# A fused cross-attention and feed-forward kernel: the order of output projection, down and up within a slot

## The chip, the cores and the metric

The kernel runs on one core of one Trainium2 chip. The time is the device time of one execution in microseconds; it is given as the median of three runs, and beside it stands one further execution that the hardware profiler recorded. The engines are named as in the profile: PE (TensorE, matrix products and transposes), DVE (VectorE), ACT (ScalarE), POOL (GpSimd) and SP (SyncE, which only issues transfers).

## The reference

The block takes `x` (16 batches of 224 tokens of width 512), a context of 16 x 750 rows of width 384 and a mask that leaves out part of the context rows:

```python
# cross attention, 8 heads of 64
q = layernorm(x) @ W_q ; k = context @ W_k ; v = context @ W_v
attn = softmax(where(mask, q k^T / 8, -max))
x = x + tanh(g_xattn) * ((attn v) @ W_o + b_o)
# feed-forward with quantised activations and weights
def bitlinear(x, w, b):              # w: ternary times one scale
    xq = act_quant(rmsnorm(x))       # per row: round(x * 127 / max|x|) / scale
    return xq @ weight_quant(w).T + b
h = gelu(bitlinear(layernorm(x), w1, b1))      # 512 -> 2048
x = x + tanh(g_ffn) * bitlinear(h, w2, b2)     # 2048 -> 512
```

The quantiser of the second product needs the largest magnitude of a whole row of `h` after the Gelu, and its rmsnorm needs the row's sum of squares.

## The kernel before, in words

**Two tilings.** Attention goes by batch: `compact_path` has a loop of 16 *slots*, one batch each (sorted by the number of context rows that the mask leaves; the first 8 slots have room for 192 rows, the last 8 for 128, `CAPS`). Everything after attention goes by *pairs*: 2 x 128 tokens, 14 pairs in all (`NPAIR`). As 224 tokens of a slot are fewer than 256, the pairs fall behind the slots: slot 9 completes no pair.

**Attention of slot s.** `scores(s, n)` for four units n (two halves of the tokens, two groups of heads): matmuls into a wide PSUM tile `sim` (line 1047), the row maximum and masking on DVE (1061, tile `nm`), Exp on ACT (1071), the reciprocal (1080) and the scaling of the probabilities `p` on POOL (1081). `turn_probs` transposes `p` on PE (1101, 1108). `weighted` multiplies with the values (1126, 1141) and ACT copies the result into `xoT` (766), a ring of four slots. Units 0 and 1 of slot s+1 are emitted at the end of slot s; units 2 and 3 in the middle of their own slot. Beside it, slot s prepares slot s+1: keys and values of its context (881, 892, 907, 918) and queries (987, 1008).

**A pair's stages.**
- `residual(i)`: POOL fetches the pair's rows of `x` into `y` (793, tag `y`, three buffers) and adds the bias (1182).
- `project(i, k)` for its two tiles k: `op`, 16 matmul records a pair (1189), then DVE adds it to `y` (1192).
- `normalise(i)`: statistics, subtraction, row maximum and quantisation on DVE (1226 to 1236), a transposing transfer on SP's queue into `xqT` (1237), some small operations and the addition of `b2` to `y` on POOL (1242, 1247).
- `up(i, k, g)`, four groups a pair: 8 matmuls each into a wide PSUM tile `hp` (1259), and DVE evicts them into `h` with scale and bias (1267). `h` has two buffers, one per k.
- `gelu(i, (k,))`: Gelu on ACT (1279), row maximum on DVE (1282), quantisation (1285, 1286), a transposing transfer into `hqT` (1288, two buffers), Square on ACT (1290), five small operations on POOL for the scale c.
- `down(i, k)`: 16 matmuls `fp` a tile (1304), DVE adds to `y` (1308), POOL stores the rows (1310).

**Order.** Each stage is a list of pieces with costs: `project_pieces` 1.8 each and then `normalise` at 0, `up_pieces` 1.8 each with `gelu` at 0 after every second, `down_pieces` 3.5 each. In a slot there are three streams: the attention of this slot, the preparation of the next one, and `flow`, which holds the stages of the pairs. `merge` (1434) emits the next piece of the stream that is least far along in its own total cost, so `flow` is spread over the slot. The emitted order is a priority: the framework then plans the queue of each engine and may put an instruction that is ready ahead of one that isn't. PSUM has two wide tiles (`ps_sim`: `sim`, `hp`, `av`) and four tiles of one bank (`ps_gen`: all else). `evict` gives a copy to DVE or ACT by a running estimate of their loads, which later stages add to.

Slots 0 and 1 have the quantisation of the weights in `flow`. From slot 2 on, before the change, `flow` is: residual(p); up of the pair projected in an earlier slot; projection and normalise of p; down of the pair whose up came just before. So slot 2 has only a projection, slots 3 to 8 have up(p-1), project(p), down(p-1), slot 9 has up(6) alone, slot 10 project(7) and down(6), and slots 11 to 15 again all three. After the loop (line 1540 and on) come the projection of pair 13, up of pair 12, and up of pair 13 woven with the downs of 12 and then 13.

Of the kernel before, what the change touches and what calls it, by code (L numbers as in the profile page):

```python
# [166 lines left out]
def flamingo_gated_kernel(  # L167
# [75 lines left out]
    with tc.If(sh.n_odd == 0) as few:  # L243
        with ExitStack() as stage:
            compact_path(stage, tc, sh, x, context, out, late_loads)
# [480 lines left out]
def compact_path(ctx, tc, sh, x, context, out, late_loads):  # L726
# [4 lines left out]
    _, J, C = context.shape  # L731
# [60 lines left out]
    def fetch_x(dst, t):  # L792
        nc.gpsimd.indirect_dma_start(
            out=dst,
            out_offset=None,
            in_=x_rows,
            in_offset=bass.IndirectOffsetOnAxis(ap=token(t), axis=0),
            bounds_check=B * S - 1,
            oob_is_err=False,
        )  # L800
# [224 lines left out]
    def norm_pieces(s):  # L1025
        pieces = []
        for t in tiles_of(s):
            if t % 2 == 0:
                pieces.append((0.0, lambda t=t: norm(t // 2)))
                if t // 2 + 2 < NTOK // 2:  # L1030
                    pieces.append((0.0, lambda t=t: fetch(t // 2 + 2)))
        return pieces
# [142 lines left out]
    def residual(i):  # L1175

        f = pairs[i] = {}
        f["y"] = y = late["rows"].tile([P, 2, D], F32, tag="y", name=f"y_{i}", bufs=3)
        for k in range(2):
            fetch_x(y[:, k, :], 2 * i + k)  # L1180
        for k in range(2):
            nc.gpsimd.tensor_tensor(y[:, k, :], y[:, k, :], sh.bo, ALU.add)

    def project(i, k):
        y = pairs[i]["y"]
        at = (2 * i + k) * P % RING
        po = gen([P, D], F32, f"op_{i}_{k}")
        for d in range(ND):
            nc.tensor.matmul(  # L1189
                po, lhsT=xoT[:, d, at : at + P], rhs=sh.wo[:, d, :], start=(d == 0), stop=(d == ND - 1)  # L1190
            )
        nc.vector.scalar_tensor_tensor(y[:, k, :], po, sh.tgates[:, 0:1], y[:, k, :], ALU.mult, ALU.add)
        load["v"] += 700
# [56 lines left out]
    def up(i, k, g):  # L1250
        f = pairs[i]
        if g == 0:
            f["h", k] = pa.tile([P, FF], F32, tag="h", name=f"h_{i}_{k}", bufs=2)
        h = f["h", k]
        ph = wide([P, 2, NB], F32, f"hp_{i}_{k}_{g}")
        for n in range(2):
            at = (2 * g + n) * NB
            for d in range(ND):
                nc.tensor.matmul(  # L1259
                    ph[:, n, :],  # L1260
                    lhsT=f["xqT"][:, k * ND + d, :],
                    rhs=w1T[:, d, at : at + NB],
                    start=(d == 0),
                    stop=(d == ND - 1),
                )
        cols = slice(2 * g * NB, 2 * (g + 1) * NB)
        nc.vector.scalar_tensor_tensor(  # L1267
            h[:, cols], ph.rearrange("t i n -> t (i n)"), f["c1", k], sh.b1[:, cols], ALU.mult, ALU.add
        )
        load["v"] += 1280  # L1270
# [29 lines left out]
    def down(i, k):  # L1300
        f = pairs[i]
        po = gen([P, D], F32, f"fp_{i}_{k}")
        for n in range(NF):
            nc.tensor.matmul(  # L1304
                po, lhsT=f["hqT", k][:, n, :], rhs=w2T[:, n, :], start=(n == 0), stop=(n == NF - 1)
            )
        y = f["y"][:, k, :]
        nc.vector.scalar_tensor_tensor(y, po, f["c2", k], y, ALU.mult, ALU.add)  # L1308
        load["v"] += 700
        nc.gpsimd.indirect_dma_start(  # L1310
            out=out_rows,
            out_offset=bass.IndirectOffsetOnAxis(ap=token(2 * i + k), axis=0),
            in_=y,
            in_offset=None,
            bounds_check=B * S - 1,
            oob_is_err=False,
        )
# [3 lines left out]
    def up_pieces(i):  # L1321
        p = []
        for k in range(2):
            p += [(1.8, lambda g=g, k=k: up(i, k, g)) for g in range(2)]
            p.append((0.0, lambda k=k: gelu(i, (k,))))
        return p

    def down_pieces(i):
        return [(3.5, lambda k=k: down(i, k)) for k in range(2)]

    def project_pieces(i):
        p = [(1.8, lambda k=k: project(i, k)) for k in range(2)]
        return p + [(0.0, lambda: normalise(i))]
# [116 lines left out]
    def weave(a, b):  # L1450

        outl = []
        ia = ib = 0
        while ia < len(a) or ib < len(b):
            if ib >= len(b) or (ia < len(a) and ia * len(b) <= ib * len(a)):
                outl.append(a[ia])
                ia += 1
            else:
                outl.append(b[ib])
                ib += 1  # L1460
        return outl
# [42 lines left out]
    projected = raised = lowered = 0  # L1504
    for s in range(B):
        other = norm_pieces(s + 2) if s + 2 < B else []
        if s + 2 < B:
            other.append((0.0, lambda s=s: gather(s + 2)))
        if s + 3 < B:
            other.append((0.0, lambda s=s: select(s + 3)))  # L1510
        if s + 1 < B:
            other += weave(context_pieces(s + 1), query_pieces(s + 1))
        flow = []
        if s < 2:
            flow = weight_pieces(s)
        else:
            complete = 256 * (projected + 1) <= S * s
            if projected == 0:
                nc.gpsimd.tensor_scalar(sh.bo, sh.bo, sh.tgates[:, 0:1], None, ALU.mult)
                nc.gpsimd.tensor_scalar(sh.b2, sh.b2, sh.tgates[:, 1:2], None, ALU.mult)  # L1520
            if complete:
                flow.append((0.0, lambda i=projected: residual(i)))
            if raised < projected:
                flow += up_pieces(raised)
                raised += 1
            if complete:
                flow += project_pieces(projected)
                projected += 1
                if lowered < raised:
                    flow += down_pieces(lowered)  # L1530
                    lowered += 1
        merge(attention_pieces(s), other, flow)
        if s == 1:

            late["stage"].close()
            late["rows"] = ctx.enter_context(tc.tile_pool(name="rows", bufs=1))
        if s + 1 < B:
            scores(s + 1, 0)
            scores(s + 1, 1)

    i = NPAIR - 1
    residual(i)
    for k in range(2):
        project(i, k)
        normalise(i, (k,))
    downs = down_pieces(i - 1) + down_pieces(i)
    for _, piece in up_pieces(i - 1):
        piece()
    for _, piece in weave(up_pieces(i), downs[:2]) + downs[2:]:
        piece()  # L1550


# [32 lines left out]
```

## Time and profile before

| | us |
|---|---|
| median of 3 runs | 762.57 (758.72 to 763.36) |
| profiled execution | 755.32 |
| its span, first to last instruction | 753.5 |
| slots 0 and 1 with all that leads in | 115.3 |
| slots 2 to 14 | 536.0 |
| slot 15 | 34.1 |
| after the loop | 68.1 |

| engine | busy us | share of the span |
|---|---|---|
| PE | 680.1 | 90% |
| DVE | 505.9 | 67% |
| ACT | 407.6 | 54% |
| POOL | 397.0 | 53% |

The slots are cut here where the matmuls of their first scores begin on PE, so a stretch ends where the next slot's `sim` starts. A group's line in the profile gives the source line, engine, operation, output and input tiles with shape and count, then busy time and the mean in ns of one, then the idle time just ahead of it on its engine and what ended it. Lines of 766 and 763 are those of `evict`, on ACT and DVE.

### The profile page before, as it was taken

The page shows a single profiled execution, that of the slowest core. Times are in us where ns is not written, and L with a number is a line of the kernel's source. Part 1 is how long each engine was busy: PE and PEld are TensorE (multiplying, and loading weights), DVE is VectorE, ACT ScalarE, POOL GpSimd, SP SyncE. Part 2 cuts the span into 40 slices and gives each one's busy share as a digit, 9 for nine tenths or more (in the row PEclk, how much of TensorE's full clock was granted, in tenths as well). Part 3 has the DMA queues.
Part 4 walks back from the last instruction along what each step waited for, and adds up shares of the span by engine and source line. Part 5 has one row for each costly group of instructions (what it writes and reads, how often), then busy time and mean ns, then how long its engine had stood idle before and what let it go on. Part 6 is the DMA issues. An engine that isn't in the chain of part 4 may idle for free.

```text
span 753.5 us, 11378 instructions
## 1 busy us (share of the span) xinstructions
PE 680.1 (90%) x3902; PEld 432.9 (57%) x3902; DVE 505.9 (67%) x1300; ACT 407.6 (54%) x960; POOL 397.0 (53%) x543
## 2 busy tenths in 40 slices
PE   4997799999999999997999999999999999988652
PEld 3875587666566566555655575666666666443221
DVE  5598765877484784665768676588594939586860
ACT  1556564384663855736657369266565656460530
POOL 6583567464564644647266564565654453536141
PEclk9998999999999999999999999999999999999887
DMA  6874031132223322222142323123122222213150
GB/s 193 314 267 156 11 90 45 15 73 56 69 47 70 82 56 57 67 57 81 28 99 67 71 67 68 32 77 80 58 57 70 56 70 57 71 28 77 35 113 31
DMA packets 87218, 58.77 MB, mean 78 GB/s; under 512 B 75488, under 2 KB 75632, under 8 KB 87024
## 3 DMA queue, kind: packets, MB, share of 16 engines
q1 hardware_dynamic: 79024, 32.00, 18.8%
q0 software_dynamic: 8128, 25.96, 11.1%
q8 instruction: 33, 0.54, 0.3%
q14 instruction: 33, 0.27, 0.1%
HBM read 32.26 MB, written 7.34 MB: 53 GB/s over the span
## 4 chain that ended last, share of the span: by engine, by line
PE 57%; DVE 12%; issue 10%; POOL 9%; DMA 5%; ACT 2%; POOLq 0%; ACTq 0%; DVEq 0%; SPq 0%
PE qp L1008 9%; PE op L1189 9%; PE fp L1304 8%; PE hp L1259 6%; PE kp L892 5%; PE sim L1047 4%; PE vp L907 4%; PE ptp L1101 3%; PE av L1126 3%; DVE a L1282 2%; POOL p L1081 2%; DVE h L1267 2%; DMA raw<-in_L_ffn_w_dram 2%; DMA hqT<-hq 2%; DVE hq L1285 1%
## 5 line engine op out<-in xcount | busy, mean ns | idle before, releaser
L1081 POOL TENSOR_TENSOR p<-p,rec 112x768 f32<-112x768 f32 (+1 forms) x64 | 84.2, 1318 | 74.8 <-DVE rec L1080 29.6
L1304 PE MATMUL fp<-w2T,hqT 128*128 128x512 fp8e4 x448 | 104.2, 387 | 13.8 <-DMA hqT<-hq 13.7
L1259 PE MATMUL hp<-w1T,xqT 128*128 128x512 fp8e4 x448 | 107.0, 383 | 8.8 <-DVE h L1267 6.2
L1071 ACT ACTIVATE p<-p,nm 112x192 f32<-112x192 f32 (+1 forms) x256 | 106.4, 419 | 11.5 <-DVE nm L1061 11.3
L1008 PE MATMUL qp<-xnT,wq_sb 128*128 128x224 f32 x512 | 104.9, 358 | 0.6 <-ACT xnT L766 0.6
L1189 PE MATMUL op<-wo_sb,xoT 128*128 128x512 f32 x224 | 103.7, 599 | 0.0
L1008 PEld LDWEIGHTS qp<-xnT,wq_sb 128*128 128x128 f32 x512 | 96.8, 193 | 6.4 <-issue 3.3
L1267 DVE SCALAR_TENSOR_TENSOR h<-hp,c,b_bc 128x1024 f32<-128x1024 f32 x56 | 71.6, 1280 | 39.9 <-PE hp L1259 37.4
L1061 DVE CUSTOM_DVE_ANT_0 p<-sim,mask 112x192 f32<-112x192 f32 (+1 forms) x256 | 67.7, 319 | 33.9 <-PE sim L1047 33.4
L1304 PEld LDWEIGHTS <-hqT 128*128 128x128 bf16 x448 | 43.3, 99 | 71.0 <-DMA hqT<-hq 16.9
L1282 DVE TENSOR_REDUCE a<-h 128x1 f32<-128x2048 f32 x28 | 63.9, 2282 | 22.4 <-ACT h L1279 22.3
L1259 PEld LDWEIGHTS <-xqT 128*128 128x128 bf16 x448 | 43.2, 98 | 57.7 <-issue 15.4
L1308 DVE SCALAR_TENSOR_TENSOR y<-fp,c,y 128x512 f32<-128x512 f32 x28 | 20.9, 746 | 76.3 <-PE fp L1304 73.0
L1310 POOL DMA_INDIRECT out_dram<-y,token x28 | 30.9, 1104 | 75.6 <-DVE y L1308 70.6
L1290 ACT ACTIVATE h<-h 128x2048 f32<-128x2048 f32 x28 | 53.4, 1907 | 22.1 <-DVE hq L1285 14.7
L1279 ACT ACTIVATE h<-h 128x2048 f32<-128x2048 f32 x28 | 53.5, 1909 | 19.6 <-DVE k L1200 10.6
L1189 PEld LDWEIGHTS op<-wo_sb,xoT 128*128 128x128 f32 x224 | 40.6, 190 | 38.9 <-issue 36.4
L892 PE MATMUL kp<-ctxT,wk_sb 128*128 128x192 f32 (+1 forms) x384 | 60.9, 306 | 0.0
L892 PEld LDWEIGHTS kp<-ctxT,wk_sb 128*128 128x128 f32 x384 | 55.2, 192 | 6.2 <-issue 4.3
L1247 POOL TENSOR_TENSOR y<-y,b_bc 128x512 f32<-128x512 f32 x28 | 36.6, 1311 | 37.9 <-DVE fx L1228 37.6
L766 ACT COPY pT<-ptp 128x448 f32<-128x448 f32 x63 | 32.7, 536 | 42.6 <-PE ptp L1101 41.3
L1101 PE MATMUL ptp<-ident,p 112*128 112x112 f32 x256 | 36.1, 268 | 17.6 <-POOL p L1081 17.5
(165 smaller groups left out, 1191.4 us busy)
## 6 DMA issues: line engine op xcount, KB each, us to landing
raw<-in_L_ffn_w_dram SPq DMA_DIRECT2D x16, 512.0 KB, 5.6
wq_sb<-in_L_xattn_W_q_dram SPq DMA_DIRECT2D x1, 1024.0 KB, 5.8
b_bc<-in_L_ffn_b_dram SPq DMA_DIRECT2D x1, 1024.0 KB, 7.8
wk_sb<-in_L_xattn_W_k_dram SPq DMA_DIRECT2D x1, 768.0 KB, 7.4
wv_sb<-in_L_xattn_W_v_dram SPq DMA_DIRECT2D x1, 768.0 KB, 8.8
wo_sb<-in_L_xattn_W_o_dram SPq DMA_DIRECT2D x1, 512.0 KB, 3.8
wo_sb<-in_L_xattn_W_o_dram SPq DMA_DIRECT2D x2, 256.0 KB, 5.6
x<-in_x_dram,token POOLq DMA_INDIRECT x28, 3.6
```

What stands on the lines that cost most here:

```text
L892: nc.tensor.matmul(pk[:, p - p0, :], lhsT=sh.wk[:, c, p * P : (p + 1) * P], rhs=st["ctxT"][:, c, :cap], start=(c == 0), stop=(c == NC - 1),)
L1008: nc.tensor.matmul(pq[:, i, :], lhsT=sh.wq[:, d, (p + i) * P : (p + i + 1) * P], rhs=st["xnT"][:, d, :], start=(d == 0), stop=(d == ND - 1),)
L1061: nc.vector.tensor_tensor_reduce(out=probs[:, h, :cap], in0=sim[:, j, i, :cap], in1=st["mask"][:, j * begin : j * begin + cap], scale=-(DH ...
L1071: nc.scalar.activation(probs[:, h, :cap], probs[:, h, :cap], AF.Exp, bias=nmax, scale=-1.0, accum_out=total[:TQ, h : h + 1],)
L1081: nc.gpsimd.tensor_tensor(probs[:, :, :cap], probs[:, :, :cap], rec[:TQ].unsqueeze(2).to_broadcast([TQ, 4, cap]), ALU.mult,)
L1101: nc.tensor.transpose(pt[:, h, :], probs[:, h, c : c + P], ident[:TQ, :TQ])
L1189: nc.tensor.matmul(po, lhsT=xoT[:, d, at : at + P], rhs=sh.wo[:, d, :], start=(d == 0), stop=(d == ND - 1))
L1259: nc.tensor.matmul(ph[:, n, :], lhsT=f["xqT"][:, k * ND + d, :], rhs=w1T[:, d, at : at + NB], start=(d == 0), stop=(d == ND - 1),)
L1267: nc.vector.scalar_tensor_tensor(h[:, cols], ph.rearrange("t i n -> t (i n)"), f["c1", k], sh.b1[:, cols], ALU.mult, ALU.add)
L1279: nc.scalar.activation(f["h", k], f["h", k], AF.Gelu)
L1282: nc.vector.tensor_reduce(amax[:, k : k + 1], h, AX.X, ALU.max, apply_absolute_value=True)
L1304: nc.tensor.matmul(po, lhsT=f["hqT", k][:, n, :], rhs=w2T[:, n, :], start=(n == 0), stop=(n == NF - 1))
```

## The change

In a slot, a pair's projection comes first, then down of the pair in front of it, then up of the pair itself. Up thus runs in the slot of its own projection. Down is no longer tied to a slot that completes a pair: it runs whenever the pair in front has been through up. After the loop, up of pair 12 is not left over, and what remains after the projection of pair 13 is emitted as down(12), up(13), down(13).

```diff
             if complete:
                 flow.append((0.0, lambda i=projected: residual(i)))
+                flow += project_pieces(projected)
+                projected += 1
+            if lowered < raised:
+                flow += down_pieces(lowered)
+                lowered += 1
             if raised < projected:
                 flow += up_pieces(raised)
                 raised += 1
-            if complete:
-                flow += project_pieces(projected)
-                projected += 1
-                if lowered < raised:
-                    flow += down_pieces(lowered)
-                    lowered += 1
         merge(attention_pieces(s), other, flow)
...
     for k in range(2):
         project(i, k)
         normalise(i, (k,))
-    downs = down_pieces(i - 1) + down_pieces(i)
-    for _, piece in up_pieces(i - 1):
-        piece()
-    for _, piece in weave(up_pieces(i), downs[:2]) + downs[2:]:
+    for _, piece in down_pieces(i - 1) + up_pieces(i) + down_pieces(i):
         piece()
```

After it, slot 2 has project(0), up(0); slots 3 to 8 have project(p), down(p-1), up(p); slot 9 has down(6) alone; slot 10 has project(7), up(7); slots 11 to 15 again have all three.

## The prediction

> **What bounds the kernel now.** First I read the busy shares, then the costliest groups with what ended their idle time.
>
> ```profile
> PE 680.1 (90%) x3902; PEld 432.9 (57%) x3902; DVE 505.9 (67%) x1300; ACT 407.6 (54%) x960; POOL 397.0 (53%) x543
> L1304 PE MATMUL fp<-w2T,hqT 128*128 128x512 fp8e4 x448 | 104.2, 387 | 13.8 <-DMA hqT<-hq 13.7
> L1259 PE MATMUL hp<-w1T,xqT 128*128 128x512 fp8e4 x448 | 107.0, 383 | 8.8 <-DVE h L1267 6.2
> L1101 PE MATMUL ptp<-ident,p 112*128 112x112 f32 x256 | 36.1, 268 | 17.6 <-POOL p L1081 17.5
> ```
>
> TensorE (PE) is busy for 90%. The next view says where the other 10% lies: busy time of every engine by stretch, cut where the scores of a slot begin (columns: stretch, length, PE, weight loads, DVE, ACT, POOL, granted clock). Shown are slots 2, 4, 7, 9, 11 and 14, then slot 15, then what follows the loop (the tail).
>
> ```profile
> 115.30:147.20 31.90, 31.80 (x203) 22.65 (x201) 21.52 (x72) 12.65 (x44) 20.28 (x23) 1.00 0.17 30
> 194.00:242.80 48.80, 46.99 (x268) 29.56 (x268) 32.62 (x77) 29.48 (x65) 27.79 (x37) 1.00 0.28 66
> 339.20:389.20 50.00, 45.06 (x251) 27.51 (x249) 30.44 (x78) 27.57 (x62) 27.27 (x36) 0.97 0.28 62
> 430.30:459.30 29.00, 27.19 (x176) 18.56 (x175) 19.62 (x56) 22.46 (x55) 16.27 (x21) 1.00 0.27 71
> 491.60:532.60 41.00, 39.94 (x226) 24.83 (x225) 32.18 (x78) 23.16 (x56) 24.13 (x35) 1.00 0.30 69
> 612.10:651.30 39.20, 39.08 (x214) 24.54 (x213) 27.30 (x67) 22.53 (x54) 18.60 (x27) 1.00 0.25 61
> 651.30:685.40 34.10, 27.48 (x146) 13.75 (x146) 25.18 (x65) 20.02 (x47) 17.49 (x23) 1.00 0.31 64
> 685.40:753.50 68.10, 38.90 (x145) 15.80 (x143) 38.37 (x51) 16.72 (x13) 19.00 (x41) 0.83 0.26 58
> ```
>
> Slots 2 to 14 last 536.0 us with 521.6 us of PE work: only 14.4 us idle in thirteen slots. Slot 15 idles for 6.6 us and the tail for 29.2, at a clock of 0.83. PE order in the tail (start, duration, count, idle before):
>
> ```profile
> 685.36 7.03 PE L1189 MATMUL op<-wo_sb,xoT 128*128 128x512 f32 x16
> 692.23 5.43 PE L1259 MATMUL hp<-w1T,xqT 128*128 128x512 fp8e4 x24
> 698.08 5.34 PE L1259 MATMUL hp<-w1T,xqT 128*128 128x512 fp8e4 x24 [0.42 <-DVE k L1200]
> 708.85 1.01 PE L1259 MATMUL hp<-w1T,xqT 128*128 128x512 fp8e4 x2 [5.44 <-DVE h L1267]
> 710.48 5.23 PE L1304 MATMUL fp<-w2T,hqT 128*128 128x512 fp8e4 x16 [0.62 <-DMA hqT<-hq]
> 715.54 3.18 PE L1259 MATMUL hp<-w1T,xqT 128*128 128x512 fp8e4 x14
> 718.86 3.63 PE L1304 MATMUL fp<-w2T,hqT 128*128 128x512 fp8e4 x16
> 731.49 8.42 PE L1304 MATMUL fp<-w2T,hqT 128*128 128x512 fp8e4 x32 [8.99 <-DMA hqT<-hq]
> ```
>
> The tail is P(13), U(12), U(13) mixed with D(12), D(13); P, U, D stand for projection, up and down of a pair. Its waits are for the two buffers of h (5.44) and for hqT (8.99). So inside the slots PE sets the pace, and after them latency does.
>
> **What the Trainium skill says.** "TensorE: Matmul & The Clock Gate", Architectural detail, says that ACT and DVE queues are strict FIFOs, so a reduce that waits for a Gelu holds all that is queued behind it on DVE. The trace agrees in kind: PE waited 5.44 us for an h eviction that stood behind others on DVE. "ScalarE: Activation LUTs", What ACT_TABLE_LOAD costs, gives 1283 ns for a load; the trace has 37 loads for Gelu and Exp of 1283 ns. "Perfetto Trace Analysis", Matmuls, wants independent groups to rotate through PSUM banks; here sims, hp and av rotate through two wide tiles and all else through four.
>
> **The change, part by part.** Prices of one pair on PE, start to start: P 6.87 us (685.36 to 692.23). An fp tile takes 3.46 (673.56 to 677.02 in slot 15), so D is 6.92. An hp group of 8 takes 1.73, so U is 6.92.
>
> Nothing is added or removed: same matmuls, Gelus, transposes and stores. U(p) moves one slot earlier, behind P(p) and D(p-1) in P's own slot.
>
> *Slot 2* gains U(0), 6.92 us; PE is 31.8 of 31.9 busy there, so all of it shows: **+6.9**. Slots 3 to 8 and 11 to 14 hold one P, U and D each, as before. Slot 9 has D(6) for U(6) and slot 10 U(7) for D(6), equal on PE.
>
> *Slot 15 and tail.* From 651.3 to the end are 102.2 us. Nominal PE work: 27.5 in slot 15 and 6.87 + 4 x 6.92 = 34.55 in the tail, 62.0. After the change U(12) runs in slot 15 where U(11) ran, and the tail is P, D, U, D: 62.0 - 6.92 = 55.1. Before, U(13) was done at 718.86, after 67.6 us, with 51.7 us of work behind it (all but D(13) and half of D(12)), so 15.9 were lost: 6.6 idle in slot 15, 6.5 idle and 2.8 of slow clock in the tail. From there to the end were 34.6 us: eviction, Gelu, reduce, quantise, transpose, D(13), store. After it, U(13) is done once 55.1 - 6.9 = 48.2 us of work and the new losses are over. Those I estimate from rows. D(11) finds hqT ready, made at the end of slot 14. U(12) waits for xqT(12): P ends 8 us into the slot, normalise is 5.7 us on DVE (sum of its rows), the transpose lands in 3.1, shared with the scores on DVE: ready at about 20 us, where work without it lasts about 17; loss 3. D(12) waits for hqT(12): Gelu 1.91, reduce 2.28, quantise 1.8, cast 0.8 and landing 4.3 are 11 us against P(13)'s 6.87; loss 4, part of which U(13) fills. I take 5, with 2 and 12 as ends (12: nothing gained on the waits of before). The closing 34.6 becomes 33: hqT of the last pair's first tile took 7.0 us to land beside the store of D(12), against a median of 4.3, and that store now lies earlier. Sum 48.2 + 5 + 33 = 86.2, against 102.2: **-16.0**. With slot 2: **-9**; ends -13 and -1.
>
> *Inside the slots*, cost zero, with covers named. (a) P opens a slot and needs y. The y fetch is not late: in slot 1 three pairs were fetched ahead; the third buffer runs about a slot ahead, and its fetch waits for a store:
>
> ```profile
> 196.82 1.07 POOL L793 DMA_INDIRECT y<-in_x_dram,token  x1 [2.02 <-DMA out_dram<-y,token]
> ```
>
> That store now falls in mid-slot, so POOL's fetch and its two adds of 1.27 us leave the slot's start, where POOL's p multiplications are due. (b) xqT(p) must be there for U(p): done near 20 us after the start by the working above, while P, D, scores and the next slot's queries and keys give PE some 24 us. SP's transpose for xqT now has hqT of U(p-1) in front of it, landed by then. (c) hqT(p) has until D(p), most of half a slot; before it had P's 7 us plus what lay between, and lost little (0.93 in slot 7). If cover (b) fails, PE waits up to 3 us a slot; in slot 10, without a D, most likely. (d) The Gelu chain of U's second tile, 1.91 + 2.28 + 1.43 + 0.80 us on ACT and DVE, ends up beside the next slot's first scores, instead of beside the middle scores. Queued behind its reduce on DVE are the row maxima, behind its Gelu on ACT the Exps; POOL's p and PE's transposes wait for these. Before, these transposes ran 9 to 13 us after the slot's start; the scores need about 8. P and D fill PE meanwhile. On POOL, U's five small operations for c (1.5 us in all) wait for ACT's Square; those of its second tile now stand about where the next slot's p stands, which at worst waits for a Square of 1.91 us. D's two stores (1.1 us of POOL each) move from the slot's end to its middle, where POOL idles. Bounds for (a) to (d) together: -8 (over half of the 14.4 idle goes, as ptp's waits for POOL shrink) to +8 when the covers hold; I take 0. (e) The greedy choice of the evicting engine sees U(0)'s load earlier; a few copies of 0.5 us go from DVE to ACT in slots 2 and 3: nothing.
>
> Against the profiled execution of 755.3 us (span 753.5) this is 746. That run lies 7.3 under the median of 762.6; I put the same difference on the median: **754**.
>
> **Rivals.**
> *Slots lose at their seam* (slower). By (d), the first scores of a slot stand behind the Gelu chain, and the two wide tiles pass from hp to sims only as DVE evicts. For it: slot 7 shows the form, ptp waiting 3.47 us for POOL's p with a Gelu chain beside it. Against: PE now has P, ready, to run there. Price: 1 to 3.5 us in each of thirteen slots; at 2, 26 - 9 = +17: 780. It decides from 9 / 13 = 0.7 us a slot.
> *The tail gives nothing that slot 2 doesn't take* (no change). D(12) waits in full for hqT(12), U(13) behind it; loss 12, so -1, and the planner's new order costs a few us: 763. For it: slot 15 lost 6.6 with the same lack of filling work. Against: two stages of latency less.
> *The slots gain too.* Scores no longer meet two Gelus in mid-slot, table loads fall, ptp's 17.5 us shrink: -9 - 8: 745.
>
> **How the numbers follow.** Chances: forecast (749 to 759) 0.45, slots gain (741 to 749) 0.15, no gain (759 to 769) 0.17, seam (769 to 795) 0.23. One per cent is 7.6 us, about what a measurement of this kernel can tell from no change. Faster than 754.9 is all of the gain case and over half of the forecast: 0.40; slower than 770.2 the seam case: 0.23; the rest 0.37. The range cuts some 0.05 below and 0.12 above: 743 to 779.
>
> **What would show it.** Right: slot 2 near 39 us, other slots within 1 us; slot 15 and tail about 86 with PE order P, D, U, D; no hp wait on h of 5 us; fewer than 37 Gelu and Exp loads. Wrong: longer slots with ptp or hp waiting, DVE's maxima behind L1282 (seam), hp waiting for xqT (cover b), or a tail of 95 us and over.

## The result and the profile after

The changed kernel takes **763.5 us** in the median of 20 runs (758.7 to 767.3), the kernel before 758.6 us in 20 runs beside them (753.0 to 763.4): a ratio of 1.0063, 95% interval 1.0040 to 1.0085. It is slightly slower; forecast was 1.1% faster (754 against 762.6). The first three runs of the kernel before, on whose median of 762.6 the forecast was put, lay high.

The profiled executions are 755.3 and 764.7 us, spans 753.5 and 763.0. The spans lie 9.5 us apart, the medians 4.9, since that of before was quicker than its median and that of after slower. The accounts below are made in these spans.

First the busy shares and groups of the page of after:

```profile
PE 686.7 (90%) x3902; PEld 438.8 (58%) x3902; DVE 509.0 (67%) x1296; ACT 392.9 (52%) x952; POOL 396.0 (52%) x543
L1304 PE MATMUL fp<-w2T,hqT 128*128 128x512 fp8e4 x448 | 110.3, 403 | 19.9 <-DMA hqT<-hq 19.9
L1259 PE MATMUL hp<-w1T,xqT 128*128 128x512 fp8e4 x448 | 104.2, 379 | 6.2 <-DMA xqT<-xq 4.8
```

The same 3902 matmuls take 6.6 us longer on PE, and `fp` waits 19.9 us for hqT instead of 13.7. `hp` waited mostly for DVE's evictions before (6.2 of 8.8); now it is mostly for xqT (4.8 of 6.2). Next the busy times by stretch, cut as before, for slots 2, 4, 7, 9, 10, 14, 15 and the tail:

```profile
114.34:157.24 42.90, 39.68 (x235) 25.83 (x233) 27.66 (x71) 17.94 (x52) 19.79 (x22) 1.00 0.09 23
203.44:250.97 47.53, 45.97 (x270) 29.46 (x269) 30.94 (x78) 26.82 (x63) 27.56 (x37) 1.00 0.31 68
346.93:395.10 48.17, 45.72 (x249) 28.20 (x247) 31.38 (x77) 24.03 (x60) 25.14 (x33) 0.93 0.27 65
435.46:469.08 33.62, 29.18 (x177) 19.38 (x176) 14.69 (x57) 19.10 (x52) 17.57 (x27) 0.90 0.32 79
469.08:506.09 37.01, 34.69 (x200) 22.41 (x199) 24.01 (x74) 16.43 (x50) 15.10 (x19) 1.00 0.07 19
626.88:667.11 40.23, 39.00 (x214) 24.29 (x213) 27.86 (x68) 22.66 (x54) 18.72 (x27) 1.00 0.25 60
667.11:701.26 34.15, 28.99 (x146) 14.09 (x146) 25.36 (x64) 19.80 (x46) 13.95 (x23) 0.95 0.25 55
701.26:763.00 61.74, 32.76 (x113) 13.13 (x111) 32.88 (x47) 13.52 (x11) 17.54 (x36) 0.77 0.27 57
```

All slots together, from both traces ("idle" is the length less PE's busy time):

| stretch | before: length (idle) | after: length (idle) | difference | forecast |
|---|---|---|---|---|
| slots 0, 1 | 115.3 | 114.3 | -0.9 | 0 |
| slot 2 | 31.9 (0.1) | 42.9 (3.2) | +11.0 | +6.9 |
| slots 3 to 8 | 283.1 (11.1) | 278.2 (7.6) | -4.9 | 0 |
| slots 9 to 11 | 102.3 (2.9) | 109.6 (7.4) | +7.3 | 0 |
| slots 12 to 14 | 118.7 (0.3) | 122.1 (3.3) | +3.3 | 0 |
| slot 15 and tail | 102.2 (35.8) | 95.9 (34.1) | -6.3 | -16.0 |
| sum | 753.5 | 763.0 | +9.5 | -9.1 |

The order of PE in the tail of after (start, duration, count, idle before):

```profile
701.26 7.03 PE L1189 MATMUL op<-wo_sb,xoT 128*128 128x512 f32 x16
709.53 3.63 PE L1304 MATMUL fp<-w2T,hqT 128*128 128x512 fp8e4 x16 [1.24 <-DMA hqT<-hq]
717.11 5.31 PE L1304 MATMUL fp<-w2T,hqT 128*128 128x512 fp8e4 x16 [3.96 <-DMA hqT<-hq]
722.26 7.07 PE L1259 MATMUL hp<-w1T,xqT 128*128 128x512 fp8e4 x32
739.39 9.88 PE L1304 MATMUL fp<-w2T,hqT 128*128 128x512 fp8e4 x32 [10.05 <-DMA hqT<-hq]
```

P, D, U, D as foreseen, but D(12) stalls twice, at a clock of 0.77 over the tail, and its second tile and D(13) run below full speed (5.31 and 9.88 us for one and two tiles, where the first tile takes 3.63).

The two slots at which late waits appear. Slot 9, which has D(6) alone, and the U of slot 10:

```profile
437.69 0.69 PE L1047 MATMUL sim<-kT,qT 64*112 64x128 f32 x8 [1.03 <-DVE h L1267]
439.13 1.54 PE L1047 MATMUL sim<-kT,qT 64*112 64x128 f32 x16 [0.75 <-DVE nm L1061]
442.62 6.34 PE L1304 MATMUL fp<-w2T,hqT 128*128 128x512 fp8e4 x16 [1.95 <-DMA hqT<-hq]
...
496.45 5.35 PE L1259 MATMUL hp<-w1T,xqT 128*128 128x512 fp8e4 x24 [2.32 <-DMA xqT<-xq]
```

In slot 9 nothing fills PE while the scores wait for the two wide tiles and D(6) for its hqT; the clock falls and the first half of D(6) takes 6.34 us instead of 3.6. In slot 10 PE has no D to run while the normalise of pair 7 goes through DVE and SP.

### The profile page after: what moved, and what is told of

Its sections match the earlier page's. It is cut to its first block, busy times and chain, and to the rows that moved or that the text cites. A ratio compares the mean times of both kernels' runs of the same rounds, so it can differ in the third digit from the quotient of the medians.

```text
span 763.0 us, 11354 instructions
## 1 busy us (share of the span) xinstructions
PE 686.7 (90%) x3902; PEld 438.8 (58%) x3902; DVE 509.0 (67%) x1296; ACT 392.9 (52%) x952; POOL 396.0 (52%) x543
## 4 chain that ended last, share of the span: by engine, by line
PE 66%; DVE 12%; DMA 6%; ACT 4%; POOL 4%; issue 3%; DVEq 0%; POOLq 0%; ACTq 0%; SPq 0%
PE fp L1304 12%; PE hp L1259 11%; PE qp L1008 10%; PE op L1189 9%; PE kp L892 5%; PE av L1126 4%; DVE a L1282 3%; PE vp L907 3%; PE sim L1047 3%; PE ptp L1101 3%; DMA hqT<-hq 2%; DMA raw<-in_L_ffn_w_dram 2%; ACT h L1279 2%; DVE h L1267 1%; DVE hq L1285 1%
## 5 line engine op out<-in xcount | busy, mean ns | idle before, releaser
L1081 POOL TENSOR_TENSOR p<-p,rec 112x768 f32<-112x768 f32 (+1 forms) x64 | 83.4, 1304 | 94.5 <-DVE rec L1080 66.7
L1304 PE MATMUL fp<-w2T,hqT 128*128 128x512 fp8e4 x448 | 110.3, 403 | 19.9 <-DMA hqT<-hq 19.9
L1071 ACT ACTIVATE p<-p,nm 112x192 f32<-112x192 f32 (+1 forms) x256 | 106.8, 420 | 29.1 <-DVE nm L1061 28.6
L1189 PE MATMUL op<-wo_sb,xoT 128*128 128x512 f32 x224 | 108.4, 624 | 7.6 <-DVE keys L833 5.1
L1259 PE MATMUL hp<-w1T,xqT 128*128 128x512 fp8e4 x448 | 104.2, 379 | 6.2 <-DMA xqT<-xq 4.8
L1304 PEld LDWEIGHTS <-hqT 128*128 128x128 bf16 x448 | 45.2, 103 | 77.0 <-DMA hqT<-hq 22.1
L1061 DVE CUSTOM_DVE_ANT_0 p<-sim,mask 112x192 f32<-112x192 f32 (+1 forms) x256 | 69.7, 314 | 15.0 <-PE sim L1047 12.0
L1259 PEld LDWEIGHTS <-xqT 128*128 128x128 bf16 x448 | 42.5, 98 | 60.1 <-issue 10.9
L1282 DVE TENSOR_REDUCE a<-h 128x1 f32<-128x2048 f32 x28 | 63.9, 2281 | 14.8 <-ACT h L1279 14.8
L1290 ACT ACTIVATE h<-h 128x2048 f32<-128x2048 f32 x28 | 53.4, 1908 | 29.7 <-DVE hq L1285 20.9
L1292 POOL TENSOR_SCALAR r<-ss 128x1 f32<-128x1 f32 x28 | 5.4, 191 | 117.5 <-ACT h L1290 116.5
L892 PEld LDWEIGHTS kp<-ctxT,wk_sb 128*128 128x128 f32 x384 | 58.0, 199 | 3.8 <-issue 1.4
L1047 PE MATMUL sim<-kT,qT 64*112 64x192 f32 (+1 forms) x512 | 51.3, 316 | 5.2 <-DVE nm L1061 4.0
L766 ACT COPY qT<-qp 128x448 f32<-128x448 f32 x30 | 15.9, 528 | 66.5 <-PE qp L1008 66.3
L1047 PEld LDWEIGHTS sim<-kT,qT 64*112 64x112 f32 x512 | 37.1, 173 | 21.8 <-issue 8.6
```

What stands on the lines that cost most here:

```text
L892: nc.tensor.matmul(pk[:, p - p0, :], lhsT=sh.wk[:, c, p * P : (p + 1) * P], rhs=st["ctxT"][:, c, :cap], start=(c == 0), stop=(c == NC - 1),)
L1047: nc.tensor.matmul(sim[:, j, i, :cap], lhsT=st["qT"][j * DH : (j + 1) * DH, p, q * TQ : (q + 1) * TQ], rhs=st["kT"][j * DH : (j + 1) * DH, ...
L1061: nc.vector.tensor_tensor_reduce(out=probs[:, h, :cap], in0=sim[:, j, i, :cap], in1=st["mask"][:, j * begin : j * begin + cap], scale=-(DH ...
L1071: nc.scalar.activation(probs[:, h, :cap], probs[:, h, :cap], AF.Exp, bias=nmax, scale=-1.0, accum_out=total[:TQ, h : h + 1],)
L1081: nc.gpsimd.tensor_tensor(probs[:, :, :cap], probs[:, :, :cap], rec[:TQ].unsqueeze(2).to_broadcast([TQ, 4, cap]), ALU.mult,)
L1189: nc.tensor.matmul(po, lhsT=xoT[:, d, at : at + P], rhs=sh.wo[:, d, :], start=(d == 0), stop=(d == ND - 1))
```

## The experiments

Ratios are to the kernel before, with their 95% intervals; slot lengths are from each kernel's one trace. All edits are to the changed kernel, unless it says otherwise. A median is of 14 to 22 executions, but of 6 for "down only beside a projection" and "all three", and of 5 for "scores first, ctxT on DVE". The rows with 757.7, with 756.5 and with 759.7 or 759.4 in the last column come from three chips, so small steps of the ratio from one of these groups to another are not read as effects.

| run | ratio | median us | before beside it |
|---|---|---|---|
| late switch | 1.0053 (1.0031 to 1.0075) | 761.5 | 757.7 |
| tail woven | 1.0028 (1.0006 to 1.0049) | 761.1 | 757.7 |
| down only beside a projection | 1.0107 (1.0073 to 1.0142) | 765.7 | 757.7 |
| kernel before, tail unwoven | 0.9994 (0.9971 to 1.0017) | 757.5 | 757.7 |
| scores first | 0.9977 (0.9956 to 0.9998) | 755.6 | 756.5 |
| early slots only | 1.0061 (1.0041 to 1.0082) | 761.3 | 756.5 |
| short maximum | 0.9991 (0.9971 to 1.0012) | 756.0 | 756.5 |
| late switch, scores first, woven | 1.0016 (0.9993 to 1.0040) | 758.0 | 756.5 |
| scores first, woven | 0.9927 (0.9903 to 0.9951) | 754.1 | 759.7 |
| scores first, ctxT on DVE | 0.9899 (0.9865 to 0.9934) | 751.8 | 759.7 |
| all three | 0.9863 (0.9824 to 0.9902) | 750.1 | 759.7 |
| kernel before, ctxT on DVE | 1.0020 (0.9993 to 1.0048) | 761.2 | 759.4 |

My theory after the traces: the work went where it was to go, and the waits that were priced at zero (seam, slot 9, slot 10, tail) ate the gain. The rivals: that the tail or slot 2 alone decides; that an early part of the change loses and a late one gains.

### Where in the program: late slots alone, early slots alone

```diff
+            if s < 10:
+                if complete:
+                    flow.append((0.0, lambda i=projected: residual(i)))
+                if raised < projected:
+                    flow += up_pieces(raised)
...
+            else:
+                if complete:
+                    flow.append((0.0, lambda i=projected: residual(i)))
+                    flow += project_pieces(projected)
...
```

> The old order up to slot 9, the new one from slot 10 on: slot 2 has only P(0), slot 9 only U(6), slot 10 has P(7), D(6), U(7), then P, D, U; the end is that of the changed kernel. Theory 'sparse slots' (the loss lies in slots 2, 9 and 10, where P and U, or D, stand without a partner to cover their latency): against the kernel before, slot 10 pays U(7) at its PE time of 6.9 us and nothing else, slots 2 and 9 are as before, slot 15 and tail keep the 6.4 us gained; sum about +1, ratio 1.000 to 1.003, and hp no longer waits for xqT. Rival 'full slots' (each slot in the new order loses at its seam): slots 11 to 14 carry a third of the loss, ratio 1.002 to 1.004 and slots 11 to 14 longer by over 1 us each. Rival 'U(0) alone' (it is the extra 6.9 us of up in an early slot and nothing else): same total as the changed kernel, 1.006, as the 6.9 us are only moved to slot 10.

Ratio 1.0053: the +1 us of 'sparse slots' missed, and by the total alone this is the changed kernel again, as the third reading has it. Slot 2 is at 31.9 and slot 9 at 29.1 again. Slot 10 now has P, D and U and is 7.7 us longer than before, of which 6.9 is the U that moved. Slots 11 to 14 are 42.6, 41.2, 40.7 and 40.2: 4.9 us longer than before. Slot 15 and the tail are 94.5, 7.7 below before. So the tail returns about what one U costs in PE time (6.92), and beside that four ordinary slots lose 4.9 us, as 'full slots' has it.

The counterpart has the new order up to slot 8, the old one from slot 9, and the old end:

```diff
+            if s < 9:
+                if complete:
+                    flow.append((0.0, lambda i=projected: residual(i)))
+                    flow += project_pieces(projected)
...
+            else:
+                if complete:
+                    flow.append((0.0, lambda i=projected: residual(i)))
+                if raised < projected:
+                    flow += up_pieces(raised)
...
-    for _, piece in down_pieces(i - 1) + up_pieces(i) + down_pieces(i):
+    downs = down_pieces(i - 1) + down_pieces(i)
+    for _, piece in up_pieces(i - 1):
         piece()
+    for _, piece in weave(up_pieces(i), downs[:2]) + downs[2:]:
+        piece()
```

> The new order up to slot 8 and the old one from slot 9 on, with the old end; slot 9 then has no share. It shows the early half of the change alone. By the windows of the changed kernel: slot 2 +11.0, slots 3 to 8 -4.9 against before; slot 9 as in the run with down beside a projection, +1.8 (31 us, though it has 7 us less PE work); slots 10 to 14 and the end as before. Sum +8, ratio 1.008 to 1.012. Rival (U(0)'s time comes back where a later slot has less to do): +4 or less, ratio under 1.006.

Ratio 1.0061, below the forecast of 1.008 and at the edge of its rival. Slot 2 is 42.9 and slots 3 to 8 sum to 275.0, 8.1 below before. Slots 10 to 14, in the old order, sum to 192.1 (192.0 before; 198.0 in the changed kernel), and slot 15 with the tail is 102.3. So of the 10.7 us that slots 9 to 14 lose in the changed kernel, the 6.0 of slots 10 to 14 belong to the new order in them, not to what came earlier, and the wide slots do gain. Slot 9 is another matter: it has no share here, 7 us less of PE work than before, and still takes 29.7 us (29.0 before), 6.6 of them idle. No half of the change wins by itself: each has to pay U's 6.9 us where it begins.

### Slot 9: no share at all

```diff
-            if lowered < raised:
+            if complete and lowered < raised:
```

> The changed kernel, but down runs only in a slot that completes a pair: slot 9 has no share at all, slot 10 has P(7), D(6), U(7). Theory 'sparse slots': slots 9 and 10 together take 63 to 65 us instead of 70.6 (61.3 in the kernel before), slot 2 stays at 43; ratio to before 0.997 to 1.001. Rival 'full slots': slots 9 and 10 gain less than 3 us as slot 9 has even less to hide its scores behind; ratio 1.005 or more.

Missed: ratio 1.0107, the slowest of all. Lines of PE in its slot 9:

```profile
434.70 0.69 PE L1047 MATMUL sim<-kT,qT 64*112 64x128 f32 x8 [0.49 <-DVE h L1267]
439.85 1.12 PE L987 MATMUL xnp<-ident,x 128*128 128x128 f32 x4 [2.17 <-DVE k L1200]
446.35 1.01 PE L1101 MATMUL ptp<-ident,p 112*128 112x112 f32 x4 [2.80 <-POOL p L1081]
447.15 5.62 PE L1008 MATMUL qp<-xnT,wq_sb 128*128 128x224 f32 x16
```

Slot 10 no longer waits for xqT, since D(6) fills PE there: its 2.3 us are gone. But without any share slot 9 idles for 6.6 us at a clock of 0.78, takes 30.8 us for 24.2 us of busy time, and slot 11 grows from 38.9 to 42.5. The three slots are 112.0, against 109.6. Behind a slot in the new order, slot 9 idles with D(6) in it (4.4 us) and without (6.6); before, with U(6), it idled for 1.8.

### The tail: its order, and DVE

```diff
-    for _, piece in down_pieces(i - 1) + up_pieces(i) + down_pieces(i):
+    downs = down_pieces(i - 1) + down_pieces(i)
+    for _, piece in weave(up_pieces(i), downs[:2]) + downs[2:]:
```

> The changed kernel, but after the loop up(13) is woven with down(12), as it was before, then down(13). If U(13) is late because it stands behind D(12) on PE, which waits for hqT(12): U(13)'s first groups run ahead of D(12)'s second tile, the end comes 3 to 4 us earlier than in the changed kernel, ratio to before about 1.002. If U(13) is late because xqT(13) itself is late (normalise of pair 13 shares DVE with the Gelu chain of U(12); in the changed kernel xqT lands at 720, U(13) starts at 722): at most 1 us, ratio 1.005 to 1.007.

Ratio 1.0028; the tail is 60.0 instead of 61.7. U(13) now may pass the second half of D(12):

```profile
707.32 3.63 PE L1304 MATMUL fp<-w2T,hqT 128*128 128x512 fp8e4 x16 [1.27 <-DMA hqT<-hq]
714.90 2.46 PE L1304 MATMUL fp<-w2T,hqT 128*128 128x512 fp8e4 x6 [3.96 <-DMA hqT<-hq]
717.60 5.85 PE L1259 MATMUL hp<-w1T,xqT 128*128 128x512 fp8e4 x24 [0.24 <-DMA xqT<-xq]
```

It passes and gains little: U(13) starts 18.6 us after the tail's beginning instead of 21.0, the moment its xqT has landed, and idle time in the tail stays at 28.3 (28.9). The ratio lies nearer to the first forecast (1.002) than to the second (1.005 to 1.007); the 1.7 us of the tail lie between the two. What is left is not PE's order. DVE has to normalise pair 13 and quantise pair 12 at the same time: in the changed kernel it works without a gap of over 0.15 us from 699.4 to 718.2, and xqT(13) lands at 719.8.

```diff
-    downs = down_pieces(i - 1) + down_pieces(i)
-    for _, piece in up_pieces(i - 1):
-        piece()
-    for _, piece in weave(up_pieces(i), downs[:2]) + downs[2:]:
+    for _, piece in up_pieces(i - 1) + down_pieces(i - 1) + up_pieces(i) + down_pieces(i):
```

> The kernel before, with only its end unwoven: up(12), down(12), up(13), down(13) in this order. It separates the order at the end from the depth of the pipeline. If D(12) ahead of U(13) makes PE wait for hqT(12) (2.7 to 4 us a tile in the changed kernel): 4 to 8 us slower than before, ratio 1.005 to 1.010. If the end is bound by DVE and the last Gelu chain whatever PE's order: within 1 us, ratio 0.999 to 1.001.

The edit is to the kernel before, and there, too, the order at the end hardly counts: 0.9994, tail 69.5 (68.1).

The last run on the tail shortens DVE's work. To the woven tail is added an edit that takes the row maximum of pair 12 over 256 of its 2048 columns, so this kernel leaves out a part of the computation:

```diff
+            part_h = h[:, :256] if i == NPAIR - 2 else h
-            nc.vector.tensor_reduce(amax[:, k : k + 1], h, AX.X, ALU.max, apply_absolute_value=True)
+            nc.vector.tensor_reduce(amax[:, k : k + 1], part_h, AX.X, ALU.max, apply_absolute_value=True)
```

> The run with the woven end, and for pair 12 alone the row maximum after Gelu is taken over 256 of 2048 columns (this leaves out part of a computation; each reduce falls from 2.28 to about 0.35 us on DVE). Theory 'DVE at the end' (U(13) starts late because normalise of pair 13 shares DVE with the Gelu chain of U(12)): xqT(13) and U(13) come 3 to 4 us earlier after the loop, the stretch after the loop falls from 60.0 to 56 to 57 us, ratio to before 0.997 to 1.000 (woven end: 1.003). Rival 'chain' (projection, statistics and transfer of pair 13 set it, whatever else is on DVE): under 1 us, ratio about 1.002.

```profile
709.63 3.41 PE L1305 MATMUL fp<-w2T,hqT 128*128 128x512 fp8e4 x15 [1.79 <-DMA hqT<-hq]
712.88 5.34 PE L1259 MATMUL hp<-w1T,xqT 128*128 128x512 fp8e4 x24
```

(The edit shifts the later line numbers by one.) One such reduce takes 0.41 us instead of 2.27; two are 3.7 us less on DVE, and the tail falls by 4.2, to 55.8. U(13) starts 15.5 us after the tail's beginning instead of 18.6. The rival (the chain of pair 13 sets it, whatever else is on DVE) falls: DVE sets the pace there.

### The seam between slots

What follows is slot 7 of the changed kernel, on DVE, from where the second unit of scores is due. L1061 is the masking with its row maximum, which frees the wide tile of a unit; L1282, 1285 and 1286 are maximum, quantisation and cast of h from U's second tile.

```profile
349.26 2.29 DVE L1282 TENSOR_REDUCE a<-h 128x1 f32<-128x2048 f32 x1 [0.46 <-ACT h L1279]
...
352.41 1.28 DVE L1285 TENSOR_SCALAR hq<-h,k 128x2048 int16<-128x2048 f32 x1
353.61 0.17 DVE L1080 RECIPROCAL rec<-sum 112x4 f32<-112x4 f32 x1
353.69 0.33 DVE L1061 CUSTOM_DVE_ANT_0 p<-sim,mask 112x192 f32<-112x192 f32 x1
353.94 2.00 DVE L1286 CAST hq<-hq 128x2048 bf16<-128x2048 int16 x1
355.86 0.34 DVE L1061 CUSTOM_DVE_ANT_0 p<-sim,mask 112x192 f32<-112x192 f32 x1
```

Three long DVE instructions, 5.6 us together, stand among the maxima. PE waits behind them with the next unit of scores:

```profile
356.27 0.98 PE L1047 MATMUL sim<-kT,qT 64*112 64x192 f32 x2 [2.45 <-DVE nm L1061]
357.18 6.48 PE L1189 MATMUL op<-wo_sb,xoT 128*128 128x512 f32 x8
```

In slots 4 to 6 it is the second half of P that waits, 1.6 to 1.8 us each, for a PSUM bank that `keys` (L833, row numbers for the gather of context) frees, behind the same instructions. This is the queue discipline that the Trainium skill states in "TensorE: Matmul & The Clock Gate", Architectural detail: DVE works strictly in order. To test it, the Gelu piece of U's second tile is held back until the first scores of the next slot have been emitted:

```diff
+    held_gelu = []
...
-                flow += up_pieces(raised)
+                flow += up_pieces(raised)[:-1]
+                held_gelu.append(lambda i=raised: gelu(i, (1,)))
...
             scores(s + 1, 0)
             scores(s + 1, 1)
+        while held_gelu:
+            held_gelu.pop()()
```

> The changed kernel, with the Gelu piece of the second tile of an up held back until the first scores of the next slot have been emitted, so that these no longer stand behind it on ACT and DVE. Theory 'seam' (in slots that lack work to cover it, and by 1.2 us in each of slots 12 to 14, PE waits because Exp and the copies on ACT stand behind the last Gelu of the slot): the idle time of slots 12 to 14 falls from 1.2 to near 0.1 us each, slot 9 loses 2 us or more of its 4.4; in all 4 to 7 us less than the changed kernel, ratio to before 0.997 to 1.001. Rival 'fill' (only PE work is missing there, the order of ACT and DVE doesn't matter): slots as before within 0.5 us, or longer because hqT comes later; ratio 1.005 or more.

Ratio **0.9977**: from slightly slower to slightly faster than before. Its slots 4 and 7:

```profile
203.58:249.50 45.92, 45.92 (x270) 29.60 (x268) 30.75 (x78) 26.70 (x63) 27.71 (x37) 1.00 0.29 70
341.37:384.46 43.09, 42.32 (x249) 26.80 (x248) 29.70 (x77) 23.90 (x60) 26.33 (x33) 1.00 0.29 72
```

With the same work, slot 4 has no idle time left and slot 7 is 5.1 us shorter: 1.7 of it wait, the rest clock (1.00 instead of 0.93). Slots 3 to 8 sum to 267.4, 10.8 below the changed kernel and 15.7 below the kernel before.

What the edit moved is less than its name says. DVE in slot 7 of this kernel:

```profile
343.70 2.29 DVE L1282 TENSOR_REDUCE a<-h 128x1 f32<-128x2048 f32 x1 [0.18 <-ACT h L1279]
...
347.22 0.35 DVE L1061 CUSTOM_DVE_ANT_0 p<-sim,mask 112x192 f32<-112x192 f32 x1
...
348.46 1.29 DVE L1285 TENSOR_SCALAR hq<-h,k 128x2048 int16<-128x2048 f32 x1
...
349.82 0.65 DVE L1286 CAST hq<-hq 128x2048 bf16<-128x2048 int16 x1
```

The Gelu and its maximum kept their places, behind the first four maxima of the scores; quantisation and cast went behind the last of the eight, and on ACT the Square behind the Exps.

The ratio fell in its range, but not for the reason given. The theory looked for the gain in slots 12 to 14, and these still idle for 1.1, 1.2 and 1.2 us (0.8, 1.2 and 1.2 without the edit); in slots 13 and 14 the order of ACT and of PE is the same with and without it. Slot 9 lost 0.6 us of idle time, not 2. The gain is in the wide slots. The next run has the late switch, the woven tail and, from slot 10 on, the held Gelu:

```diff
+            if s < 10:
...
+                    flow += up_pieces(raised)
...
+            else:
...
+                    flow += up_pieces(raised)[:-1]
+                    held_gelu.append(lambda i=raised: gelu(i, (1,)))
...
+    for _, piece in weave(up_pieces(i), downs[:2]) + downs[2:]:
```

> A candidate: the old order up to slot 9, from slot 10 the new one with the held Gelu, and the woven end. Theory 'seam' with 'sparse slots': late switch alone is +4.0; the held Gelu takes 1.1 us from each of slots 11 to 14, the woven end 1.5: -2, ratio 0.996 to 0.999. If holding the Gelu gives nothing: ratio 1.002 to 1.004.

1.0016, between its two forecasts: slots 11 to 14 are at 40.7, 40.7, 40.7 and 40.2, where the late switch alone had 42.6, 41.2, 40.7 and 40.2. The hold helps in slots 11 and 12 and does nothing in slots 13 and 14.

### The narrow slots: a copy behind ScalarE's queue

The start of slot 14 in the changed kernel, ACT and PE in order of time:

```profile
629.88 1.90 ACT L1279 ACTIVATE h<-h 128x2048 f32<-128x2048 f32 x1
631.79 1.28 ACT L1071 ACT_TABLE_LOAD   x1
633.08 0.40 ACT L1071 ACTIVATE p<-p,nm 112x128 f32<-112x128 f32 x1
...
634.64 0.35 ACT L766 COPY ctxT<-ctxp 128x256 f32<-128x256 f32 x1
```

```profile
635.04 3.70 PE L1189 MATMUL op<-wo_sb,xoT 128*128 128x512 f32 x8 [1.23 <-ACT ctxT L766]
```

The transposes `ctxp` were done on PE by 628. Their copy into `ctxT` was given to ACT, as in the kernel before, but here it stands behind Square, Gelu, a table load and four Exps; the second half of P wants its PSUM bank. The edit, on top of the held Gelu, takes the copy off ACT:

```diff
-            evict(st["ctxT"][:, c0:c1, :cap], pt, (c1 - c0) * cap)
+            if s >= 11:
+                nc.vector.tensor_copy(st["ctxT"][:, c0:c1, :cap], pt)
+            else:
+                evict(st["ctxT"][:, c0:c1, :cap], pt, (c1 - c0) * cap)
```

> The held Gelu chain again, and the copies of the context's transposes (ctxT) of slots 11 to 15 put on VectorE instead of the engine that the running sums choose. Theory: with the new order the output projection's second half waits 1.23 us a slot in slots 12 to 14, because the PSUM bank that it takes is freed by a ctxT copy that stands on ScalarE behind Square, Gelu, a table load and four Exps. Off ScalarE the wait goes: idle of slots 12 to 14 from 1.1 or 1.2 to below 0.3 us each, each slot about 1 us shorter, 3 us in all. Rival: the same bank is late anyway, since VectorE at that time is on the maxima of the scores, or TensorE meets another wait behind it: slot lengths stay at 40.2 to 40.7 with the idle time under another name.

Ratio 0.9899. Slots 12, 13 and 14 of this kernel:

```profile
539.47:578.89 39.42, 39.42 (x224) 24.81 (x223) 27.36 (x73) 22.76 (x54) 22.86 (x33) 1.00 0.28 65
578.89:618.17 39.28, 39.28 (x218) 24.67 (x217) 27.73 (x70) 22.66 (x54) 18.69 (x27) 1.00 0.30 61
618.17:657.25 39.08, 39.08 (x214) 24.32 (x213) 28.37 (x70) 22.05 (x52) 18.62 (x27) 1.00 0.30 61
```

PE is busy from end to end in all three: 117.8 us, against 121.6 with the held Gelu alone. In each of them just two copies changed engine. Slot 11, whose own copies are moved as well, became 1.3 us longer; its D waits 1.67 us for hqT. The rival (another wait takes its place) fell for slots 12 to 14 and holds in slot 11. The copy without the held Gelu was not run.

The control is the same edit on the kernel before:

> The kernel before, with nothing but the ctxT copies of slots 11 to 15 on VectorE. Theory: the copy on ScalarE held TensorE only in the new order; in the old one slots 12 to 14 idle by 0.03 to 0.12 us each, so there is nothing to win: 0.998 to 1.002 of the kernel before, slots 12 to 14 at 39.8, 39.7 and 39.2 within 0.5 us. Rival: the copies gain by themselves in any order, and the gain of the three edits together has nothing to do with the change: 0.993 to 0.996, these slots 1 us shorter each.

1.0020, interval 0.9993 to 1.0048; slots 12 to 14 are 39.8, 39.7 and 39.2 as before. In the old order the copy is worth nothing: in slot 14 four Exps and no Gelu stand ahead of it, and P does not open the slot. That wait was made by the change.

### The parts together

Held Gelu and woven tail:

> The two edits that helped alone, together: the Gelu chain of U's second tile is held back until the next slot's first scores, and at the end U(13) and D(12) alternate. If each acts in its own place (the wide slots; the tail) the gains add: some 6 us against the changed kernel from the first, 1.5 from the second, so 0.995 to 0.997 of the kernel before, a tail near 60 us and slots 3 to 8 near 267.5 in sum. If the tail is limited by DVE and the clock whatever its order, the second gives nothing on top: 0.9977 again.

0.9927, better than expected; slots 3 to 8 sum to 267.7 and the tail is 59.7, so in the trace the gains add as forecast. The ratio beyond that isn't explained by these stretches. The 0.9977 of the held Gelu alone was measured on another chip than this ratio and the 0.9899 with the copy, so the two steps are read from the traces.

Held Gelu, copy on DVE, woven tail:

> All three: held Gelu chain, ctxT copies of slots 11 to 15 on VectorE, U(13) alternating with D(12) at the end. If the three act apart, the sum of their gains: slots 3 to 8 near 267.5, slots 12 to 14 near 118.5, tail near 60, and 0.991 to 0.995 of the kernel before. If ScalarE's copy is not what held TensorE, the same as without the second edit, 0.995 to 0.998.

**0.9863**, 750.1 us: faster than both kernels, and the lowest median of the study, though its interval overlaps that of the run without the woven tail. Slot 13 and the tail of it:

```profile
578.91:618.19 39.28, 39.28 (x218) 24.66 (x217) 27.73 (x70) 22.69 (x54) 18.73 (x27) 1.00 0.29 61
690.36:749.50 59.14, 31.68 (x113) 12.51 (x111) 32.73 (x47) 13.53 (x11) 17.71 (x36) 0.84 0.28 59
```

Against the span of the kernel before: slot 2 +11.0, slots 3 to 8 -15.6, slots 9 to 11 +8.9, slots 12 to 14 -0.9, slot 15 and tail -9.9, and +2.6 in slots 0 and 1, which run the same order in every kernel here and still lasted from 113.0 to 117.9: -4.0. The medians differ by 9.7; the profiled execution of the kernel before was 3 us quicker than its median, that of this kernel 1.3 slower than its own. Beside slot 2, what is left on the table is slots 9 to 11. Whether a held Gelu would help the old order too was not run, so it isn't shown that this result needs the new one.

## Why the prediction was wrong

- **The step that failed** is the tail's: "Those I estimate from rows", with 5 us lost before U(13) ends. U(13) ended at 729.33, 62.2 us after slot 15 began: 48.2 of work, as forecast, and **14.0** lost, above even the upper bound of 12. Of these, 10.4 are waits: 2.66 for the hqT of D(11), 1.12 for `p`, 1.38 for an eviction of `h`, 1.24 and 3.96 for the hqT of D(12). Another 3.4 are slow clock, which the sum left out, though it counts 2.8 of it before. "D(11) finds hqT ready" was false: its two tiles landed 7.6 and 16.5 us into slot 15. "part of which U(13) fills" was false as well: xqT(13) landed at 719.8, when D(12)'s second wait was over, because normalise(13) and the Gelu chain of pair 12 share DVE, as the run with a short maximum shows. The 3 us put on xqT(12) did not come. The closing term of 33 was right (33.7). So a latency chain was taken as one that later work would cover, and the stage that left it, U(12), gave back only about its time on PE: -6.3.
- **The whole miss** in the spans is 18.6 us (-9.1 forecast, +9.5 measured): 9.7 in slot 15 and the tail, 4.1 in slot 2, 7.3 in slots 9 to 11 and 3.3 in slots 12 to 14, less 4.9 in slots 3 to 8 and 0.9 in slots 0 and 1. So "*Inside the slots*, cost zero" failed too, in the narrow slots.
- **Slot 2**, +6.9 forecast, +11.0 measured. The direction and the 6.9 hold; 3.2 of waits came on top (1.83 `hp` for xqT, 1.39 `ptp` for `p`). Cover (b) counted on "P, D, scores and the next slot's queries and keys", and slot 2 has no D. The remaining 0.9 is PE work pulled forward, half of which slot 3 gives back.
- **Cover (b)** was named to fail "in slot 10, without a D, most likely", at up to 3 us: it did, 2.32; among the full slots only slot 11 waited for xqT, 0.67. I had left it out of the sum. That was right as a reading and wrong as a sum.
- **Cover (d)**, the seam, failed in its mechanism: PE did not have "P, ready, to run there", since the second half of P needs a PSUM bank whose copy stands in the same queues. The size was below the 2 us of the rival: 1.6 to 1.8 in slots 4 to 6, 2.45 and slow clock in slot 7, 0.8 to 1.2 in slots 12 to 14. In the wide slots it was outweighed: before, each of slots 4 to 7 already idled for 1.5 to 4.9, and over the whole kernel PE's waits of `ptp` for POOL's `p` fell from 17.5 to 5.5, as in the rival in which the slots gain. The held Gelu shows what the seam itself cost there: 7.5 to 10.8 us, most of it wait and clock (five traces with this order in slots 3 to 8 have 275.0 to 278.2 us there, the one with the held Gelu alone 267.4).
- **"Slot 9 has D(6) for U(6) ..., equal on PE"** was true in work and wrong in time. D needs an hqT that was made at the seam just ahead of it, U an xqT made a slot earlier: +4.6 in that slot, 2.6 of it waits and the rest slow clock.
- **Covers (a), (c), (e).** The y fetch held up nothing (a). hqT was late in slots 9 and 15 and in the tail, nowhere else (c). The greedy choice moved some copies of slot 2 from DVE to ACT, as foreseen, and no wait of PE shows them (e). The copies of `ctxT` in slots 12 to 14 were on ACT before as well; what changed is what stands ahead of them, and that belongs to (d).
- **The rivals.** None occurred whole. The result lies where the second put it (763), in part by luck, since that stands on a base that lay high; the tail gave less than slot 2 took, with part of the first (the seam) and of the third (wide slots gain). Fewer table loads came as foreseen, 25 instead of 37; what they were worth was not measured apart.
- **Base and working.** The base was also high: put on a median of 758.6, the same forecast would have been near 750. With losses of 2 and 12 the sum gives -12 and -2, not the -13 and -1 of the prediction. And the eviction for which PE waited 5.44 us did not stand behind others on DVE: DVE idled for 1.46 us ahead of it, until ACT's Square had freed the buffer of `h`.

## What to carry to other kernels

A stage taken out of a tail that waits for latency returned about its own engine time here (6.3 and 7.7 us for 6.92); a shorter chain on DVE returned 4.2 for 3.7. So follow the last two pairs engine by engine (here DVE) before pricing a fill. When a stage with a long in-order tail (Gelu, maximum, quantise, cast) is moved to a seam, list every short instruction queued behind it on each engine, copies that free PSUM banks included; getting those out from behind it was worth more here than the reordering itself. A slot without its usual filling work, at either end or in mid-program, needs an account of its own.

## What the hardware showed that I had not expected

**A short wait can halve PE's clock for several microseconds.** Slot 7 of the changed kernel, by microsecond (the third column from the end is the granted clock):

```profile
354.00:355.00 1.00, 0.00 (x0) 0.00 (x0) 1.00 (x3) 1.00 (x1) 1.00 (x1) 1.00 0.00 0
355.00:356.00 1.00, 0.00 (x0) 0.00 (x0) 1.00 (x2) 1.00 (x3) 0.39 (x1) 0.99 0.00 0
356.00:357.00 1.00, 0.73 (x2) 0.44 (x2) 1.00 (x5) 1.00 (x6) 0.00 (x0) 0.50 0.00 0
...
361.00:362.00 1.00, 1.00 (x2) 0.42 (x2) 0.00 (x0) 0.00 (x0) 0.92 (x2) 0.50 0.00 0
362.00:363.00 1.00, 1.00 (x2) 0.34 (x1) 0.00 (x0) 0.00 (x0) 0.92 (x3) 0.59 0.00 0
```

After 2.45 us of wait the clock stands at a half for some 6.8 us, though PE is busy again from 356.3: the eight `op` matmuls take 6.48 instead of 3.70. In slot 6 a wait of 1.80 us was followed by some 3.4 us at a half, and `op` took 5.40. With the held Gelu, slot 7 waits for 0.8 us and the clock there stays at 1.00, in all four traces that have it in the wide slots.

The stretches at a half have fixed lengths: the 92 of them in the fourteen traces that ended before the program did last 3.41, 6.83, 10.24 or 13.65 us, multiples of 3.41. The length of a wait doesn't settle which one follows, or whether any does. The same 2.45 us in slot 7 was followed by 6.83 us in three traces with this order and by 3.41 in two. The 1.80 us of slot 6 was followed by none in the other four of these. A wait of 1.47 us in slot 5 of the old order was followed by 3.41 us in two traces and by none in that of the kernel before. And 3.57 us in slot 7 of the run with late switch, scores first and woven tail was followed by none. The Trainium skill ("TensorE: Matmul & The Clock Gate", HAM oscillation) warns of gaps above some 3.4 us; here 1.47 was enough, not every time. So a wait of 1.5 to 2.5 us costs between its own length and more than twice that (2.45, and half of 6.83 on top).

**DVE slows beside POOL.** The cast in the seam took 2.00 us, where the same shape elsewhere in this kernel has a median of 0.68; POOL's multiplication of `p` ran from 353.93 to 355.40, over most of it. With the held Gelu the same cast in slot 7 runs clear of that multiplication and takes 0.65. "GPSIMD Engine Reference", 1. Specifications, says that POOL shares its SBUF interfaces with DVE; this trace agrees in kind, and the cause was not tested by a run of its own.
